# A fused decoder layer: the product of k and q stated at a later step, a sequence's prologue over two passes, a power one pass on

## The chip, the cores and the metric

The kernel is one program on one core of a Trainium2 chip. The metric is the device time of one execution in microseconds. The core has a matmul engine (TensorE; the profile tells its matmuls, PE, from its weight loads, PEld), three other compute engines (VectorE or DVE, ScalarE or ACT, GpSimd or POOL) and SyncE (SP), which here issues most of the DMAs. Every engine works through its own queue in order; engines wait for one another by semaphores.

## The reference

A decoder layer on x of shape (4, 512, 512): three residual blocks, each on a layer norm of x without weights. The first is a gated delta rule with 16 heads of 128, the second a cross attention to a context of 256 rows, the third an attention with a mixture of eight experts. The change lies in the first alone:

```python
q = _causal_conv(x @ Wq.T, cw_q, cb_q)      # four taps along the time, bias, silu
k = _causal_conv(x @ Wk.T, cw_k, cb_k)
v = _causal_conv(x @ Wv.T, cw_v, cb_v)
g = jnp.exp(-jnp.exp(A_log)[None, None, :] * jax.nn.softplus(a + dt_bias[None, None, :]))
beta = jax.nn.sigmoid(b)
q = _l2norm(q.reshape(Bb, Ss, H, DK))
k = _l2norm(k.reshape(Bb, Ss, H, DK))

def step(Sstate, inputs):
    q_t, k_t, v_t, g_t, beta_t = inputs
    retrieved = jnp.einsum('bhkv,bhk->bhv', Sstate, k_t)
    error = v_t - g_t[..., None] * retrieved
    update = k_t[..., :, None] * (beta_t[..., None] * error)[..., None, :]
    Snew = g_t[..., None, None] * Sstate + update
    o_t = jnp.einsum('bhkv,bhk->bhv', Snew, q_t)
    return (Snew, o_t)
```

a and b are two further projections of x to 16 columns each. The output o is normalised, gated by silu(x Wg) and projected by Wo.

## The kernel before, in words

The recurrence is computed in chunks of 128 time steps. A sequence of 512 steps has four chunks (TB), and the 16 heads are taken two at a time (HG = 2, so NHG = 8 groups). Four sequences times eight groups make 32 **passes**, numbered m from 0 to 31; "even" and "odd" below are by m.

Each pass m needs five pieces of work, each a Python generator that yields after every step, so that the pieces can be interleaved as the program is written out:

- `stage1(m)` (L534): the keys and queries of the two heads. k's projection and convolution (`conv`, L509: four matmul steps of L515, on ACT the last tap and the bias at L523, on DVE the three other taps at L526, on ACT Silu at L529), k's transposes (L558), the sums of its squares (L563) and their power on POOL (`rk`, L570), the decay matrix `em` (a scan on DVE at L579, scaled on ACT by `scale`, L397), k times k on PE (L588) and from it `at` (DVE, L591), which goes to DRAM. Then q: for each of the two heads its projection and convolution, `qg` (q times a row of decays, POOL, L602), q squared (ACT, L605), and the **product** of k and q: four pairs of matmuls (L612), multiplied by `em` on DVE into `pt` (L614). Last come the column sums of q squared (PE, L621; ACT, L623), which go by DMA into `rq` (L627), k decayed by chunk (`kdec`, L631 and L397) and the **power** of `rq` on POOL (L635, L636).
- `stage2_inverse(m)` (L649): a triangular inverse by elimination, 31 steps of two instructions each (L657, L658), on DVE for even m and on POOL for odd m, and its way through DRAM (L663 to L671).
- `stage2_values(m)` (L691): v's projection, convolution and transposes (L703, L705), the gate's projections (`conv` with m = 3, ACT at L519), and at its start the DMA of `rq` to DRAM (`r_d`, L696).
- `stage3(m)` (L721): the recurrence over the chunks: L735 to L769 finish the inverse; then per chunk L787 (k times state), L789 (`r`), L796 and L798 (`u`), L806, L809 and L811 (the next state), L814 and L816 (the output `po`). `stage3` reads `r_d` back (L773).
- `output(m)` (L841): the product with Wo (L860), summed over groups (L865).

`prologue(b)` (L405) prepares a sequence once: for each of its four tiles of 128 rows the layer norm (`layernorm`, L125: statistics on DVE at L131 and L132, `rsqrt` at L122 on DVE and L123 on POOL, normalising on DVE at L137), four transposes on PE (L427) and a copy on ACT (L428); then the two small projections (L435), softplus and the decays by a long row of small DVE operations (L438 to L483) with exponentials on ACT, and two rows of decays to DRAM (L493), which `stage1` reads back.

The main loop (L963) interleaves them. While `stage3(m)` takes its fifteen steps, after each of them one **turn** of the rest is taken: one step of `output(m - 1)`, two steps of `stage1(m + 2)`, one of `stage2_values(m + 1)`, two calls of `inversions` (the inverse of m + 1, and from about turn 10 on the first steps of that of m + 2), and in passes 4, 12 and 20 one step of the next sequence's prologue. What is left when `stage3(m)` is done is run to its end. For DVE and POOL the order so written is the order in which they work (L947: a manual schedule for these two); for PE and ACT the program's builder may move an instruction ahead of one written before it.

A step of `stage1` without work of its own ("yield" twice in a row) only puts distance between what stands before and behind it. Its 29 yields before fill the fifteen turns. In turn 9 q's first convolution ends, and in turn 10 its product is stated; in turns 11 and 12 the second head's projection and convolution, in turn 13 its product; in turn 14 the sums of squares, in turn 15 the end. PSUM tiles `pb` of the projections, transposes and products come from one pool of four.

Of the kernel before, what the change touches and what calls it, by code (L numbers as in the profile page):

```python
# [31 lines left out]
F32 = mybir.dt.float32  # L32
# [66 lines left out]
def decoder(ctx: ExitStack, tc: tile.TileContext, a: dict, out: bass.AP):  # L99
# [73 lines left out]
    def run(*gs):  # L173
        for g in gs:
            for _ in g:
                pass

    def turns(*gs):

# [146 lines left out]
    with ExitStack() as st:  # L326
# [78 lines left out]
        def prologue(b):  # L405

            x = []

            def load(c):

                t = w2.tile([P, D], F32, name="xa", bufs=4) if b == 0 and c > 1 else w2.tile([P, D], F32, name="x_in", bufs=2)
                nc.sync.dma_start(t, x_t[:, b * TB + c, :])
                x.append(t)

            for c in range(TB if b == 0 else 2):
                load(c)
            yield
            yield
            for c in range(TB):
                t = x[c]  # L420
                run(layernorm(t.unsqueeze(1), t.unsqueeze(1), small))
                if c == 0:
                    xnT = s2.tile([P, KD, S], F32, name="xnT", bufs=2)
                    seqs[b] = [xnT]
                tp = p_b.tile([P, KD, P], F32, name="pb")
                for kd in range(KD):
                    nc.tensor.transpose(tp[:, kd, :], t[:, kd * P : (kd + 1) * P], ident)  # L427
                nc.scalar.copy(xnT[:, :, c * P : (c + 1) * P], tp)  # L428
                if b > 0 and c + 2 < TB:
                    load(c + 2)  # L430
                yield
            pab = p_b.tile([P, TB, 32], F32, name="pb")
            for c in range(TB):
                for kd in range(KD):
                    nc.tensor.matmul(pab[:, c, :], xnT[:, kd, c * P : (c + 1) * P], wab[:, kd, :], start=kd == 0, stop=kd == KD - 1)  # L435
            g_a, lg, beta, gam, ngam, gend, gall = (seq.tile([P, H1, TB], F32, name=n) for n in ("g_a", "lg", "beta", "gam", "ngam", "gend", "gall"))
            nc.scalar.activation(beta, pab[:, :, 16:32].rearrange("p i h -> p h i"), AF.Sigmoid)
            nc.vector.tensor_tensor(g_a, pab[:, :, 0:16].rearrange("p i h -> p h i"), along(dtb, TB), ALU.add)  # L438


            y, z, w = (small.tile([P, H1, TB], F32, name=n, bufs=1) for n in ("sp_y", "sp_z", "sp_w"))
            nc.vector.scalar_tensor_tensor(y, g_a, -1.0, g_a, ALU.mult, ALU.min)
            nc.scalar.activation(y, y, AF.Exp)
            yield
            nc.vector.tensor_scalar(w, y, 2.0, None, ALU.add)
            nc.vector.reciprocal(w, w)
            nc.vector.tensor_tensor(z, y, w, ALU.mult)
            nc.vector.tensor_tensor(w, z, z, ALU.mult)
            nc.vector.tensor_scalar(y, w, 1.0 / 17, None, ALU.mult)
            for n in (15, 13, 11, 9, 7, 5, 3):  # L450
                nc.vector.scalar_tensor_tensor(y, y, 1.0 / n, w, ALU.add, ALU.mult)
                if n in (11, 5):
                    yield
            nc.vector.scalar_tensor_tensor(y, y, 1.0, z, ALU.add, ALU.mult)
            nc.vector.tensor_scalar(y, y, 2.0, None, ALU.mult)
            nc.vector.scalar_tensor_tensor(y, g_a, 0.0, y, ALU.max, ALU.add)
            nc.vector.scalar_tensor_tensor(y, y, -1.0, along(alog, TB), ALU.mult, ALU.mult)

            nc.vector.tensor_scalar(lg, y, -200.0, None, ALU.max)
            yield  # L460

            lgf = lg.rearrange("p h i -> p (h i)")
            pg = p_b.tile([P, 3, H1 * TB], F32, name="pb")
            for n, m in enumerate((C_UP, C_LO, C_ONE)):
                nc.tensor.matmul(pg[:, n, :], tab_a[:, m, :], lgf, start=True, stop=True)
            for n, dst in enumerate((gam, gend, gall)):
                nc.scalar.activation(dst.rearrange("p h i -> p (h i)"), pg[:, n, :], AF.Exp)
            nc.vector.tensor_scalar(ngam, gam, -1.0, None, ALU.mult)
            yield

            nc.vector.tensor_scalar(y, lg, -87.0, None, ALU.max)
            nc.vector.tensor_scalar(z, y, float(np.log2(np.e)), None, ALU.mult)
            nc.vector.tensor_scalar(z, z, MAGIC, MAGIC, ALU.add, ALU.subtract)
            nc.vector.scalar_tensor_tensor(y, z, -0.693145751953125, y, ALU.mult, ALU.add)
            nc.vector.scalar_tensor_tensor(y, z, -1.42860677e-06, y, ALU.mult, ALU.add)
            yield
            nc.vector.tensor_scalar(w, y, 1.0 / 5040, None, ALU.mult)
            for n in (720, 120, 24, 6, 2, 1):
                nc.vector.scalar_tensor_tensor(w, w, 1.0 / n, y, ALU.add, ALU.mult)
            n2 = small.tile([P, H1, TB], mybir.dt.int32, name="n2", bufs=1)  # L480
            nc.vector.tensor_scalar(n2, z, 127.0, None, ALU.add)
            nc.vector.tensor_scalar(n2, n2, 23, None, ALU.logical_shift_left)
            nc.vector.scalar_tensor_tensor(w, w, 1.0, n2.bitcast(F32), ALU.add, ALU.mult)  # L483
            yield

            tp = p_b.tile([H1 * TB, 2, P], F32, name="pb")
            nc.tensor.transpose(tp[:, 0, :], w.rearrange("p h i -> p (h i)"), ident)
            nc.tensor.transpose(tp[:, 1, :], gam.rearrange("p h i -> p (h i)"), ident)
            gr = w2.tile([P, TB * 64], F32, name="Y6").rearrange("p (n t) -> p n t", n=2)[0 : H1 * TB]
            nc.scalar.copy(gr, tp)  # L490
            nc.gpsimd.memset(gr[:, 0, 0:1], 0.0)
            for n in range(2):
                nc.sync.dma_start(g_d[b, n], gr[:, n, :])  # L493
            seqs[b] += [beta, gam, ngam, gend, gall]
            yield
# [38 lines left out]
        def stage1(m):  # L534
# [59 lines left out]
            load_blocks(m, ats)  # L594
            mb = rows(1)

            qg, pt, sq = [], [], []
            for p in range(HG):
                q = s1.tile([P, S], F32, name="qh")
                yield from conv(b, hg, p, 0, wq, q)  # L600
                g = live.tile([P, S], F32, name="qg", bufs=6)
                nc.gpsimd.tensor_tensor(g, q, mb[p], ALU.mult)  # L602
                qg.append(g)
                t = w2.tile([P, S], F32, name="cv", bufs=5)
                nc.scalar.activation(t, q, AF.Square)  # L605
                sq.append(t)
                yield
                yield
                pq = p_b.tile([P, TB, P], F32, name="pb")
                for c in range(TB):  # L610
                    cs = slice(c * P, (c + 1) * P)
                    nc.tensor.matmul(pq[:, c, :], kT[p][:, cs], q[:, cs], start=True, stop=True)  # L612
                t = live.tile([P, TB, P], F32, name="pt", bufs=6)
                nc.vector.tensor_tensor(t, pq, em[p], ALU.mult)  # L614
                pt.append(t)
                yield
            load_weights(m + 1, 0)

            pss = p_b.tile([P, S], F32, name="pb")
            for p in range(HG):  # L620
# [5 lines left out]
            for p in range(HG):  # L626
                nc.sync.dma_start(rq[p * P // HG : (p + 1) * P // HG, :], sr[p * 32 : p * 32 + 1, :].rearrange("o (n k) -> o n k", k=HG * TB))  # L627
            yield
            kd_ = []
            for p in range(HG):  # L630
                t = live.tile([P, TB, P], F32, name="kdec", bufs=4)  # L631
                scale(t, kt[p], ke, p)
                kd_.append(t)
                yield
            nc.gpsimd.tensor_scalar(rq, rq, 1e-24, None, ALU.max)  # L635
            nc.gpsimd.tensor_tensor(rq, rq, mhalf[:, 0 : HG * TB], ALU.pow)  # L636
            keys[m] = (kT, kd_, qg, pt, nr, rq)

        inverses, begun, joined = {}, {}, {}
# [51 lines left out]
        def stage2_values(m):  # L691
# [1 line left out]
            b, hg = divmod(m, NHG)  # L693
            nr, rq = keys[m][4:]
            wv, wg = weights.pop((m, 2)), weights.pop((m, 3))
            nc.sync.dma_start(r_d[m % SLOTS].rearrange("c t -> (c t)").rearrange("(n k) -> n k", k=HG * TB), rq)  # L696
            v_, gs = [], []
            for p in range(HG):
                t = yield from conv(b, hg, p, 2, wv, None)
# [4 lines left out]
                v = w2.tile([P, TB, P], F32, name="vn", bufs=4)  # L704
                nc.vector.tensor_tensor(v, tp, along(nr[:, p * TB : (p + 1) * TB], P), ALU.mult)  # L705
                v_.append(v)
                yield
            load_weights(m + 1, 2)
            for p in range(HG):
# [253 lines left out]
        for m in range(NP):  # L963
# [21 lines left out]
            if m + 1 < NP:  # L985
                rest.append((stage2_values(m + 1), 1))
                rest.append((inversions(m, turn), 2))
            if (m + 4) % NHG == 0 and (m + 4) // NHG < B:
                rest.append((prologue((m + 4) // NHG), 1))
            rest = turns(*rest)  # L990
            for _ in stage3(m):
                next(rest, None)
# [576 lines left out]
```

## Time and profile before

| | us |
|---|---|
| median of three runs | 3905.05 (3903.72 to 3906.9) |
| the profiled execution | 3901.65 |
| its span, first to last instruction | 3899.8 |
| start up to the first pass (first matmul of L735) | 156.0 |
| a pass, most of them | 61.3 to 61.7 |
| passes 4, 12 and 20, with a prologue | 90.5 to 90.6 |
| passes 8, 16 and 24 | 64.7 to 64.8 |
| pass 30, which has no more `stage1` | 39.1 |

The passes follow one another from 156 us on, and pass 31, the last, begins at 2132.0 us; the cross attention, the attention and the experts follow and are not touched. The page's row of PE's clock gives in tenths what the throttle granted over the span; slices 5, 10 and 15 hold the prologues:

```
PE   5898799897898899897898789999999999899897
PEclk8899899998999998999999799999999999999898
```

In the views below a row of a group of instructions reads: line, engine, operation, tile written and tiles read, shapes, count, then busy us and mean ns, then the idle time of the engine just before these instructions and what ended it. A row of a stretch reads: from and to, its length, the busy time of PE, PEld, DVE, ACT and POOL with the number of instructions, the granted clock (1.00 is full speed), the share of the DMA engines and GB/s. A row of the timeline reads: start, duration, engine, line, operation, tiles, count, and in brackets the idle time before it and its cause.

### The profile page before, as it was taken

The numbers are of one execution on the slowest core, as the hardware profiler recorded it, in microseconds if no ns is written. First come the engines' busy times: TensorE is split into PE (matmuls) and PEld (weight loads), VectorE is DVE, ScalarE is ACT, GpSimd is POOL, SyncE is SP. The second block draws the span as 40 slices with busy tenths as digits, with TensorE's granted clock in tenths as the row PEclk, the third lists the DMA queues.
The fourth block names the chain that finished last, engine by engine and source line by source line (L and its number), as shares of the span: only waits on it lengthen the run. The fifth ranks groups of instructions, "written<-read, shape, count | busy, mean of one in ns | idle before, by whom it ended". The sixth has DMA issues, their size and how long they took to land. (4 is left out here: it accounts for less than half of the span.)

```text
span 3899.8 us, 48830 instructions
## 1 busy us (share of the span) xinstructions
PE 3462.8 (89%) x16466; PEld 1967.7 (50%) x16466; DVE 2187.2 (56%) x4923; ACT 1566.2 (40%) x4379; POOL 1387.2 (36%) x1941
## 2 busy tenths in 40 slices
PE   5898799897898897899898789999999999899897
PEld 3555455554555554555555445555555555554343
DVE  5566566754765566566754446655665556554111
ACT  3444444443443444444443324444444444444121
POOL 1453453455255533553455222212211211211442
PEclk8899899998999998999999799999999999999898
DMA  5333233432334332334333155445544444456344
GB/s 151 99 107 112 84 94 107 129 94 87 104 100 127 96 101 86 108 93 131 103 97 110 43 176 159 138 135 155 166 143 144 144 142 133 139 169 213 79 83 92
DMA packets 391880, 465.56 MB, mean 119 GB/s; under 512 B 128451, under 2 KB 242115, under 8 KB 391440
## 3 DMA queue, kind: packets, MB, share of 16 engines
q1 hardware_dynamic: 380080, 438.03, 36.7%
q0 software_dynamic: 10112, 21.58, 2.9%
q8 instruction: 132, 2.16, 0.2%
q10 hardware_dynamic: 1440, 2.84, 0.2%
q14 instruction: 116, 0.95, 0.1%
HBM read 401.76 MB, written 64.81 MB: 120 GB/s over the span
## 5 line engine op out<-in xcount | busy, mean ns | idle before, releaser
L515 PE MATMUL pb<-xnT,w 128*128 128x512 f32 x2048 | 962.6, 608 | 18.4 <-DVE at L591 12.7
L515 PEld LDWEIGHTS pb<-xnT,w 128*128 128x128 f32 x2048 | 381.2, 197 | 426.8 <-issue 396.0
L526 DVE SCALAR_TENSOR_TENSOR cv<-pb,pp,cv 128x510 f32<-128x510 f32 (+2 forms) x576 | 423.5, 744 | 36.1 <-ACT cv L523 24.4
L1111 PE MATMUL pb<-c_q,hT 128*128 128x512 f32 x768 | 362.3, 610 | 10.9 <-DMA c_q<-in_c_wk_dram 3.3
L523 ACT ACTIVATE cv<-pb,pp 128x512 f32<-128x512 f32 x192 | 148.7, 775 | 374.2 <-PE pb L515 374.1
L658 POOL TENSOR_TENSOR iT<-iT,iW 32x31 f32<-32x31 f32 (+15 forms) x496 | 272.5, 549 | 38.9
L657 POOL TENSOR_TENSOR iW<-iA,iT 32x31 f32<-32x31 f32 (+15 forms) x496 | 246.3, 497 | 50.3 <-DMA iA<-at_d 9.6
L860 PE MATMUL pb<-wot,og 128*128 128x512 f32 x512 | 262.2, 636 | 1.5 <-issue 1.5
L602 POOL TENSOR_TENSOR qg<-qh,row 128x512 f32<-128x512 f32 x64 | 81.9, 1280 | 460.9 <-ACT qh L529 460.9
L1217 PE MATMUL pw<-c_o,oT 128*128 128x512 f32 x512 | 241.8, 603 | 2.9 <-DVE oT L1209 2.9
L1111 PEld LDWEIGHTS pb<-c_q,hT 128*128 128x128 f32 x768 | 144.3, 196 | 169.6 <-issue 152.3
L1183 ACT ACTIVATE e<-pb,nm,rq 128x128 f32<-128x128 f32 (+3 forms) x256 | 156.8, 618 | 140.5 <-DVE nm L1181 108.0
L570 POOL TENSOR_TENSOR rk<-ss,mhalf 128x8 f32<-128x8 f32 x32 | 87.1, 2722 | 346.9 <-DVE ss L569 346.0
L865 DVE TENSOR_TENSOR xa<-pb,xa 128x512 f32<-128x512 f32 x112 | 76.8, 686 | 219.2 <-PE pb L860 219.0
L657 DVE TENSOR_TENSOR iW<-iA,iT 32x31 f32<-32x31 f32 (+15 forms) x496 | 178.9, 361 | 28.4 <-DMA iA<-at_d 17.5
L658 DVE TENSOR_TENSOR iT<-iT,iW 32x31 f32<-32x31 f32 (+15 forms) x496 | 181.6, 366 | 17.1
L274 POOL TENSOR_SCALAR x_e<-x_e 128x1024 f32<-128x1024 f32 x64 | 67.4, 1053 | 331.2 <-ACT x_e L269 232.1
L1207 PE MATMUL po<-eT,val 128*128 128x512 f32 x320 | 170.2, 625 | 6.8 <-ACT eT L1205 3.8
L612 PE MATMUL pb<-qh,kT 128*128 128x128 f32 x512 | 97.3, 349 | 88.0 <-ACT qh L529 88.0
L1177 PE MATMUL pb<-kT,qT 128*128 128x256 f32 (+3 forms) x576 | 162.7, 409 | 0.8 <-ACT x_e L269 0.8
L269 ACT ACTIVATE x_e<-pb,nm 128x256 f32<-128x256 f32 x256 | 118.0, 476 | 96.5 <-DVE nm L266 96.5
L1039 POOL TENSOR_TENSOR rope_s<-q,tab 128x128 f32<-128x128 f32 x64 | 35.2, 550 | 316.2 <-DVE q L1141 270.1
(331 smaller groups left out, 6576.1 us busy)
## 6 DMA issues: line engine op xcount, KB each, us to landing
c_o<-in_c_wo_dram SPq DMA_DIRECT2D x128, 512.0 KB, 4.1
c_q<-in_c_wq_dram SPq DMA_DIRECT2D x128, 512.0 KB, 4.7
w<-in_a_w_dram SPq DMA_DIRECT2D x124, 512.0 KB, 3.9
row<-g_d SPq DMA_DIRECT2D x64, 512.0 KB, 3.5
at_d<-at SPq DMA_DIRECT2D x64, 256.0 KB, 2.2
T<-t_d SPq DMA_DIRECT2D x32, 512.0 KB, 4.1
X<-x_d SPq DMA_DIRECT2D x32, 512.0 KB, 5.2
wot<-in_a_wo_dram SPq DMA_DIRECT2D x32, 512.0 KB, 3.6
```

The source lines that it names most:

```text
L269: nc.scalar.activation(e[:, n, :], ps[r][:, g, :], AF.Exp, bias=nm[:, n : n + 1], accum_out=ssum[:, n : n + 1])
L515: nc.tensor.matmul(pj, wt[:, kd, p * P : (p + 1) * P], xnT[:, kd, :], start=kd == 0, stop=kd == KD - 1)
L523: nc.scalar.activation(ac, pj, AF.Identity, bias=cb[:, m, h : h + 1], scale=cw[:, m, h, 3:4])
L526: nc.vector.scalar_tensor_tensor(ac[:, j:], pj[:, : S - j], cw[:, m, h, 3 - j : 4 - j], ac[:, j:], ALU.mult, ALU.add)
L657: eng.tensor_tensor(u, A[:, i, i + 1 :].unsqueeze(2).to_broadcast([nb, n, w]), T[:, i, :w].unsqueeze(1).to_broadcast([nb, n, w]), ALU.mult)
L658: eng.tensor_tensor(T[:, i + 1 :, :w], T[:, i + 1 :, :w], u, ALU.add)
L860: nc.tensor.matmul(pw, og[p][:, c * P : (c + 1) * P], wot[:, p, :], start=p == 0, stop=p == HG - 1)
L1111: nc.tensor.matmul(pj, hT[:, kd, :], w[:, kd % 2, :], start=kd == 0, stop=kd == KD - 1)
L1177: nc.tensor.matmul(ps[:, m, k * P : (k + w) * P], qT[g][:, n + m, :], kT[:, g, j : j + w, :], start=True, stop=True)
L1183: nc.scalar.activation(e[n + m][:, :nk], ps[:, m, :nk], AF.Exp, bias=nm[:, n + m : n + m + 1], scale=rq, accum_out=es[:, n + m : n + m + 1])
L1207: nc.tensor.matmul(po, val[:, g, :], eT, start=k == 0, stop=k == c)
L1217: nc.tensor.matmul(pw, oT[:, h + m, :], w[:, m, :], start=g == 0 and h + m == 0, stop=g == 3 and h + m == 3)
```

## The change

It has four parts.

1. In `stage1` the product becomes a function and is stated at another place. The first head's stands in the second head's convolution, behind its projection and ahead of its taps (the third step of `conv`); the second head's stands behind the column sums of q squared. The two steps without work go, so `stage1` has 26 yields in place of 29. `kdec` is stated one head at a time, the first ahead of the column sums, and the load of q's next weights comes two turns earlier.
2. The power of `rq` moves out of the end of `stage1(m)` into `stage2_values(m)`, behind the first head's v, that is into turn 5 of the next pass, and the DMA of `rq` to `r_d` moves with it from turn 1.
3. For the sequences after the first, the prologue's steps are drawn out: the statistics of a tile, its normalising and its transposes stand in different turns, and the small DVE operations are cut into more steps. For the first sequence the statistics of all four tiles stand ahead of the first normalising.
4. The prologue runs in passes 4, 12 and 20 only as long as `stage3` has turns left (`within`, which stops when the list `turn` is emptied) and goes on in passes 5, 13 and 21. With one step a turn the four tiles' transposes are stated in the first pass, and everything from L435 on in the second, up to its turn 12.

```diff
+    def within(g, turn):
+
+        while turn and next(g, g) is not g:
+            yield
...
             yield
             yield
+            norms_of = [layernorm(t.unsqueeze(1), t.unsqueeze(1), small) for t in x]
+            for g in norms_of[: TB if b == 0 else 1]:
+                next(g)
+            if b:
+                yield
             for c in range(TB):
                 t = x[c]
-                run(layernorm(t.unsqueeze(1), t.unsqueeze(1), small))
+                run(norms_of[c])
+                if b:
+                    yield
+                    if c + 1 < TB:
+                        next(norms_of[c + 1])
+                    yield
...
                 if b > 0 and c + 2 < TB:
                     load(c + 2)
+                    norms_of.append(layernorm(x[c + 2].unsqueeze(1), x[c + 2].unsqueeze(1), small))
                 yield
...
             for n in (15, 13, 11, 9, 7, 5, 3):
                 nc.vector.scalar_tensor_tensor(y, y, 1.0 / n, w, ALU.add, ALU.mult)
-                if n in (11, 5):
+                if n in (15, 11, 7, 3):
                     yield
...
             for n in (720, 120, 24, 6, 2, 1):
                 nc.vector.scalar_tensor_tensor(w, w, 1.0 / n, y, ALU.add, ALU.mult)
+                if n in (24, 1):
+                    yield
...
-            qg, pt, sq = [], [], []
+            qh, qg, pt, sq, kd_ = [], [], [], [], []
+
+            def product(p):
+                pq = p_b.tile([P, TB, P], F32, name="pb")
+                for c in range(TB):
+                    cs = slice(c * P, (c + 1) * P)
+                    nc.tensor.matmul(pq[:, c, :], kT[p][:, cs], qh[p][:, cs], start=True, stop=True)
+                t = live.tile([P, TB, P], F32, name="pt", bufs=6)
+                nc.vector.tensor_tensor(t, pq, em[p], ALU.mult)
+                pt.append(t)
+
+            def decayed(p):
+                t = live.tile([P, TB, P], F32, name="kdec", bufs=4)
+                scale(t, kt[p], ke, p)
+                kd_.append(t)
+
             for p in range(HG):
                 q = s1.tile([P, S], F32, name="qh")
-                yield from conv(b, hg, p, 0, wq, q)
+                c = conv(b, hg, p, 0, wq, q)
+                yield from itertools.islice(c, 2)
+                if p:
+                    product(0)
+                yield from c
+                qh.append(q)
...
                 sq.append(t)
                 yield
-                yield
-                pq = p_b.tile([P, TB, P], F32, name="pb")
-                for c in range(TB):
-                    cs = slice(c * P, (c + 1) * P)
-                    nc.tensor.matmul(pq[:, c, :], kT[p][:, cs], q[:, cs], start=True, stop=True)
-                t = live.tile([P, TB, P], F32, name="pt", bufs=6)
-                nc.vector.tensor_tensor(t, pq, em[p], ALU.mult)
-                pt.append(t)
-                yield
             load_weights(m + 1, 0)
+            decayed(0)
+            yield
...
             yield
-            kd_ = []
-            for p in range(HG):
-                t = live.tile([P, TB, P], F32, name="kdec", bufs=4)
-                scale(t, kt[p], ke, p)
-                kd_.append(t)
-                yield
-            nc.gpsimd.tensor_scalar(rq, rq, 1e-24, None, ALU.max)
-            nc.gpsimd.tensor_tensor(rq, rq, mhalf[:, 0 : HG * TB], ALU.pow)
+            product(1)
+            yield
+            decayed(1)
+            yield
             keys[m] = (kT, kd_, qg, pt, nr, rq)
...
-            nc.sync.dma_start(r_d[m % SLOTS].rearrange("c t -> (c t)").rearrange("(n k) -> n k", k=HG * TB), rq)
...
                 v_.append(v)
+                if p == 0:
+                    nc.gpsimd.tensor_scalar(rq, rq, 1e-24, None, ALU.max)
+                    nc.gpsimd.tensor_tensor(rq, rq, mhalf[:, 0 : HG * TB], ALU.pow)
+                    nc.sync.dma_start(r_d[m % SLOTS].rearrange("c t -> (c t)").rearrange("(n k) -> n k", k=HG * TB), rq)
                 yield
...
+
             if (m + 4) % NHG == 0 and (m + 4) // NHG < B:
-                rest.append((prologue((m + 4) // NHG), 1))
+                coming = prologue((m + 4) // NHG)
+                rest.append((within(coming, turn), 1))
+            elif (m + 3) % NHG == 0 and (m + 3) // NHG < B:
+                rest.append((coming, 1))
```

## The prediction

> **What bounds the kernel now.** I read the page first, then the granted clock by stretches, then TensorE's waits over the delta rule's passes, then the order of time inside a pass. The kernel before has 32 passes (one sequence and two heads each); in the trace a pass begins at the first matmul of L735, at 733.9, 795.5, 857.2 us and so on. The page:
>
> ```profile
> span 3899.8 us, 48830 instructions
> PE 3462.8 (89%) x16466; PEld 1967.7 (50%) x16466; DVE 2187.2 (56%) x4923; ACT 1566.2 (40%) x4379; POOL 1387.2 (36%) x1941
> L612 PE MATMUL pb<-qh,kT 128*128 128x128 f32 x512 | 97.3, 349 | 88.0 <-ACT qh L529 88.0
> ```
>
> TensorE (PE) is the bound, and the product of k and q waits 88.0 us for q's Silu. The chain that ended last covers only the closing DMAs and says nothing here. The waits of PE from 156 to 2093 us (total, times, longest):
>
> ```profile
> PE pb L612 <- ACT qh L529: 77.2, 42, 2.7
> PE pb L427 <- DVE x_in L137: 49.8, 12, 7.4
> PE ps L806 <- ACT u L798: 36.8, 24, 2.7
> PE ps L787 <- DVE state L811: 21.7, 20, 1.4
> ```
>
> The change touches the first two. Four passes (length; PE, PEld, DVE, ACT and POOL busy; clock; DMA): odd, even, even with a prologue, the odd one behind it:
>
> ```profile
> 733.90:795.50 61.60, 55.69 (x301) 32.45 (x301) 42.47 (x87) 26.28 (x77) 19.64 (x30) 0.97 0.38 112
> 795.50:857.20 61.70, 55.19 (x298) 32.39 (x298) 34.94 (x70) 26.20 (x77) 39.70 (x59) 0.97 0.35 103
> ...
> 918.60:1009.20 90.60, 69.44 (x353) 43.16 (x352) 46.70 (x115) 36.88 (x92) 41.43 (x64) 0.87 0.27 83
> 1009.20:1071.60 62.40, 56.20 (x301) 32.67 (x302) 44.63 (x91) 26.09 (x77) 21.21 (x31) 0.95 0.34 101
> ```
>
> A prologue makes its pass 28.9 us longer than an even one and its clock 0.87. Where the clock goes:
>
> ```profile
> 772.00:775.70 3.70, 0.75 (x4) 0.56 (x4) 3.63 (x8) 0.60 (x1) 0.00 (x0) 1.00 0.70 166
> 775.70:779.40 3.70, 3.62 (x17) 3.62 (x18) 1.17 (x3) 1.70 (x5) 2.46 (x6) 0.54 0.80 193
> ...
> 832.10:837.05 4.95, 2.34 (x16) 1.96 (x16) 4.84 (x9) 1.42 (x4) 3.41 (x3) 1.00 1.03 242
> 837.05:840.60 3.55, 3.55 (x17) 3.55 (x18) 1.09 (x3) 1.66 (x4) 2.50 (x2) 0.54 0.51 147
> ...
> 942.40:949.20 6.80, 6.73 (x29) 3.99 (x29) 0.83 (x3) 1.58 (x4) 2.67 (x5) 0.50 0.12 39
> ```
>
> Behind the wait at the first product (2.46 us in both passes) PE runs at 0.54 for some 3.6 us: the product takes 1.98 us, the one at 788.9 only 1.11. So that wait costs 2.46 + 0.46 x 3.6 = 4.1 us.
>
> **Part A: the product is stated later.** Nothing is added or removed on PE, ACT or DVE; the order changes. Before, q's second projection (eight matmuls of L515) stands behind the first product; now it stands ahead of it, and the second product stands behind the sums of squares (L621). The 27 passes 0 to 29 without a prologue have the 4.1 us: 15 odd, 12 even. Even ones also wait 0.76 at the second product. What is late next:
>
> Odd pass, from the product at L787 (772.57): L787 0.6, eight matmuls at 5.36/12 = 0.45 each 3.6, L796 0.6, the first product 1.1: 778.5. Then on DVE pt (L614) 0.69 and three taps 2.3, on ACT Silu 0.63 and Square 0.63, handovers 0.3: 783.0. PE meanwhile has the transposes of v 0.65, half a gate projection 1.8, L806/L814/L816 1.3: 782.3. If L621 is next it waits 0.7, if the gate's other half (1.8), not at all. With L621 (1.05) and that half done PE stands at 785.1 to 785.9; before, it ends that half at 787.67 and L621 would be done at 788.7. Gain 2.8 to 3.6; I take 3.0, near the lower since what is stated first usually goes first.
>
> Even pass: DVE is held up by something that the change leaves, the landing of the next inverse's blocks:
>
> ```profile
> 836.85 0.60 DVE L789 SCALAR_TENSOR_TENSOR r<-ps,ngam,vn 128x128 f32<-128x128 f32 x2
> 837.05 1.83 PE L612 MATMUL pb<-qh,kT 128*128 128x128 f32 x8 [2.46 <-ACT qh L529]
> ...
> 842.34 0.18 DVE L657 TENSOR_TENSOR iW<-iA,iT 32x31 f32<-32x31 f32 x1 [1.02 <-DMA iA<-at_d]
> ```
>
> Two steps of the inverse stand there ahead of pt and q's taps in DVE's written order: 842.34 + 0.9 + 0.69 + 2.3 + 0.62 + 0.63 + handovers 0.3 = 847.8. PE, from 834.59: 3.6 + 0.6 + 0.65 + 1.1 + 1.8 + 1.3 + 1.8 = 10.9, so 845.5, and waits 2.3. What is then left (L621 1.05, L787 0.6, second product 1.1, gate 3.6, L796 0.6, L814/L816 0.9: 7.9) ends at 855.7; before, the next pass began at 857.2. Gain 1.5.
>
> A = 15 x 3.0 + 12 x 1.5 = 63 us. Bounds: 15 x 2.5 + 12 x 0.5 = 44 if handovers take twice as long and the blocks land 1 us later; 15 x 3.6 + 12 x 3.2 (both waits gone, clock unchanged) = 92.
>
> **Part B: the prologue over two passes.** Of the 28.9 us, PE's work at full clock is 16 transposes 2.6 (four take 0.65 at L558), L435 3.65, L465 0.78, L487/L488 0.3: 7.3. The other 21.6 is waits and slow clock. The first tile:
>
> ```profile
> 934.68 0.15 DVE L122 TENSOR_SCALAR rsq<-ln_mv 128x1 f32<-128x1 f32 x1
> 940.94 0.56 POOL L123 TENSOR_TENSOR ln_rs<-rsq,mhalf 128x1 f32<-128x1 f32 x1
> 941.54 0.88 DVE L137 TENSOR_SCALAR x_in<-x_in,ln_mv,ln_rs 128x512 f32<-128x512 f32 x1 [6.71 <-POOL ln_rs L123]
> 942.47 1.11 PE L427 MATMUL pb<-tab,x_in 128*128 128x128 f32 x4 [7.38 <-DVE x_in L137]
> ```
>
> The power stands on POOL behind the inverse, DVE waits 6.71 for it, PE 7.38, and then 3.34, 3.06, 2.76 for the other tiles. Now normalising is a turn (61.6/15 = 4.1 us) behind the statistics and the transposes one or two more. POOL's lag there falls too: the power of q's sums (L635, L636: 0.25 + 1.67 + gaps 0.16 = 2.1 us), which stood ahead of this in the same unbroken run of POOL, goes behind it. 940.94 - 2.1 = 938.8 is ahead of the turn's end (in an undisturbed even pass DVE ends turn 4 at 818.1, 22.6 into the pass, here 941.2). So these waits go.
>
> What comes: the second half (L435 to L491) lands in the odd pass behind, whose DVE has no break from 742.7 to 766.2. It adds some 8.6 us of small DVE operations (0.2 to 0.25 each, L451's seven 1.8); PE brings 3.65 + 0.78 = 4.4 of its own, so up to 4.2 shows; I take 4. In the even pass two powers of 0.56 stand ahead of rk (L570): 1. Then 28.9 - 7.3 - 5 + 1.5 (A's gain, which this pass now has too) = 18.1, x 3 = 54 us. Bounds: no cover, 9.7 in place of 5: 40; all but 1 covered: 66.
>
> **Moved at no cost.** The power (now turn 5 of the next pass): in odd passes POOL idles 22 us ahead of rk; in even ones it stays within the same run ahead of rk, so rk's time stands; without that cover it is 2.1 x 12 = 25 us. The DMA of it to r_d moves past wot's load on SP; behind it in turn 5 is only at's store, not ready before 830.8. The row is read a pass later. q's weights are loaded two turns earlier, once L515 is done. kdec (L397) runs at 846.2 already, ahead of its place in the text.
>
> Rule against row: POOL's rk takes 1.65 us alone and 3.61 beside DVE's scan, whose own 1.17 does not grow; so a power beside DVE's two-input steps costs POOL time, not DVE. [...]
>
> **Part C: the start.** Prologue 0 has twelve steps in place of eight beside k's projections; on DVE the second k's taps now stand ahead of the exponentials (35.3 to 38.8), which end up to 5 us later. Against it two product waits there (6.36 and 3.94). Net between -5 and +10; I take 0.
>
> **Sum.** 63 + 54 + 0 = 117; 3901.65 (span 3899.8 and 1.85 around it) - 117 = 3785. The median of the runs is 3.4 above the profiled execution: 3788. All bounds: gain 79 to 168, so 3737 to 3826.
>
> **Rivals.**
> 1. The wait only moves: L621 stands one turn behind Square as the product stood one turn behind Silu. PE's order is also not wholly the text's (kdec), so it may fall back. Then A is 12 x 0.76 = 9: 3905 - 9 - 54 = 3842. Against it: eight matmuls (3.6 us) now stand between. 15%.
> 2. The prologue's waits move into the odd pass; only its slow clock comes back: L860 11.37 against 7.83, L427 3.95 against 2.6, L796 and L767 0.9: 5.8 x 3 = 17, so 3905 - 63 - 17 = 3825. 12%.
> 3. The slow clock stays, as other waits remain in those turns (L806 2.68, L787 1.40): 27 x 1.65 = 45, so 3833. Against it: behind the lone 2.68 at 832.1 the clock was 1.00. [...] 8%.
> 4. Slower: in DVE's written order pt now stands ahead of q's taps. If PE reaches the product late, taps 2.3, Silu and Square 1.25, state, r and u 1.7 and six handovers 0.6 lie bare where nothing fills PE: 5.9 + slow clock 1.6 = 7.5 in 27 passes, 203. Against the waits removed (27 x 4.4 = 119) and B 54: 3934. It decides from 6.4 us a pass; the eight matmuls make PE late by 3.6 only. 9%.
> 5. Gains and losses cancel: 3905, 3%.
>
> The forecast has 53%; its own range is 3745 to 3825. The range 3737 to 3850 takes in rivals 1 to 3. This kernel's runs lie within 3.2 us; 0.2% (8 us) is what can be told from no change: faster 88%, within 3%, slower 9%.
>
> **What will show it.** PE's wait at the product near 0, no 0.54 stretch behind it; a wait at L621 under 1 us in odd and about 2 in even passes; odd passes 58.6, even ones 60.2; a prologue's two passes about 133 in place of 153; L427's waits gone after the start. Wrong if L621 or L787 takes over the 2.46, or if the odd pass behind a prologue exceeds 70.

## The result, and the profile after

The changed kernel takes 3777.2 us (median of four runs, 3771.8 to 3784.6) against 3906.0 us for the kernel before in the same session: a ratio of 0.9672 with a 95% interval of 0.9654 to 0.9689. The forecast was 3788 us with a range of 3737 to 3850. The profiled execution took 3776.1 us, 125.9 us less in its span than the one before.

The page after (span; then busy us, share of the span and number of instructions of each engine):

```profile
span 3773.9 us, 48783 instructions
PE 3437.1 (91%) x16466; PEld 1917.6 (51%) x16466; DVE 2189.5 (58%) x4923; ACT 1559.3 (41%) x4379; POOL 1383.9 (37%) x1941
```

DVE, ACT and POOL are as busy as before to 7 us. PE's busy time fell by 25.7 us though it runs the same 16466 matmuls: part of the gain is not idle time but a faster clock (granted on the mean 0.98 in place of 0.95 below). Passes 2 to 29 as one stretch, before and after (length; PE, PEld, DVE, ACT, POOL busy; clock; DMA):

```profile
270.20:2092.90 1822.70, 1601.96 (x8482) 943.16 (x8481) 1132.92 (x2311) 765.91 (x2201) 855.37 (x1262) 0.95 0.35 102
262.30:1969.80 1707.50, 1580.89 (x8485) 896.96 (x8487) 1134.91 (x2311) 759.73 (x2201) 852.92 (x1262) 0.98 0.36 109
```

Of the 115.2 us that went here, 94.1 were idle time of PE and 21.1 busy time. The waits of PE over the passes (147.9 to 1969.8 us; total, times, longest):

```profile
PE ps L836 <- ACT u L828: 47.5, 24, 3.6
PE pb L576 <- ACT kT L547: 17.1, 30, 2.8
PE pb L621 <- ACT qh L547: 15.5, 14, 1.2
PE pb L533 <- DVE at L609: 13.4, 3, 4.5
PE pb L481 <- DVE lg L475: 12.5, 3, 5.0
```

L621 is the product (L612 before): 15.5 us of waits are left of 77.2. The prologue's transposes, 49.8 before, are gone from the list. The largest wait is now one that the change left alone (L836, L806 before) and that grew from 36.8 to 47.5. The four passes that were shown before, an odd one, an even one, one with a prologue and the odd one behind it (length; PE, PEld, DVE, ACT, POOL busy; clock; DMA):

```profile
694.20:751.90 57.70, 55.02 (x297) 30.54 (x296) 43.37 (x90) 25.93 (x77) 19.44 (x29) 1.00 0.41 123
751.90:812.50 60.60, 55.87 (x297) 31.82 (x296) 35.05 (x67) 26.04 (x77) 40.15 (x60) 0.97 0.35 105
870.30:933.00 62.70, 57.46 (x317) 33.24 (x320) 37.67 (x81) 27.60 (x80) 42.05 (x64) 0.97 0.39 115
933.00:1003.40 70.40, 63.30 (x341) 37.69 (x341) 52.41 (x125) 34.99 (x89) 19.29 (x30) 0.93 0.27 79
```

The odd pass is 3.9 us shorter, with the clock at 1.00 all through. The two passes of a prologue together take 133.1 in place of 152.9. Within the odd pass (PE and ACT alone; start, duration, engine, line, what):

```profile
732.83 0.75 PE L817 MATMUL ps<-state,kT 128*128 128x128 f32 x4 [0.53 <-DVE state L841]
733.41 2.74 PE L533 MATMUL pb<-xnT,w 128*128 128x512 f32 x6
735.35 0.63 ACT L547 ACTIVATE qh<-cv 128x512 f32<-128x512 f32 x1 [4.74 <-DVE cv L544]
...
737.71 1.06 PE L621 MATMUL pb<-qh,kT 128*128 128x128 f32 x8
...
741.75 1.04 PE L652 MATMUL pb<-cv,tab_a 128*32 128x512 f32 x2
...
743.78 1.05 PE L652 MATMUL pb<-cv,tab_a 128*32 128x512 f32 x2
```

The same product and sums of squares in the odd pass before:

```profile
775.78 1.98 PE L612 MATMUL pb<-qh,kT 128*128 128x128 f32 x8 [2.46 <-ACT qh L529]
...
791.68 1.05 PE L621 MATMUL pb<-cv,tab_a 128*32 128x512 f32 x4
```

Two of the second projection's eight matmuls even went ahead of L817; the other six fill the time until Silu ends at 735.98, and the product runs in 1.06 us and not in 1.98. The two heads' sums of squares (L652, L621 before) wait for nothing, since two of the gate's matmuls stand between them. But this parting has a price. Standing together, the four matmuls of the sums took 1.05 us; parted, each head's two take as long alone. PE's and PEld's busy time on that line in the odd pass, before and after:

```profile
733.90:795.50 61.60, 1.05 (x4) 0.14 (x4) 0.97 0.38 112
694.20:751.90 57.70, 2.09 (x4) 0.27 (x4) 1.00 0.41 123
```

So each pass costs PE 1.04 us more, 29.1 us over passes 2 to 29. All other matmuls there took 50 us less (21.1 and 29.1), at a granted clock of 0.98 in place of 0.95.

### The profile page after: what moved, and what is told of

Same layout as the page of the kernel before. It is cut to its first block, busy times and chain, and to the rows that moved or that the text cites. A ratio compares the mean times of both kernels' runs of the same rounds, so it can differ in the third digit from the quotient of the medians.

```text
span 3773.9 us, 48783 instructions
## 1 busy us (share of the span) xinstructions
PE 3437.1 (91%) x16466; PEld 1917.6 (51%) x16466; DVE 2189.5 (58%) x4923; ACT 1559.3 (41%) x4379; POOL 1383.9 (37%) x1941
## 5 line engine op out<-in xcount | busy, mean ns | idle before, releaser
L533 PE MATMUL pb<-xnT,w 128*128 128x512 f32 x2048 | 974.5, 610 | 18.4 <-DVE at L609 13.9
L533 PEld LDWEIGHTS pb<-xnT,w 128*128 128x128 f32 x2048 | 373.6, 195 | 407.8 <-issue 384.2
L890 PE MATMUL pb<-wot,og 128*128 128x512 f32 x512 | 252.3, 616 | 2.0 <-issue 1.5
L685 DVE TENSOR_TENSOR iT<-iT,iW 32x31 f32<-32x31 f32 (+15 forms) x496 | 192.0, 387 | 17.1
L402 ACT ACTIVATE em<-em,ee 128x128 f32<-128x128 f32 x256 | 78.3, 388 | 178.3 <-POOL ee L590 108.5
```

What stands on the lines that cost most here:

```text
L533: nc.tensor.matmul(pj, wt[:, kd, p * P : (p + 1) * P], xnT[:, kd, :], start=kd == 0, stop=kd == KD - 1)
L685: eng.tensor_tensor(T[:, i + 1 :, :w], T[:, i + 1 :, :w], u, ALU.add)
L890: nc.tensor.matmul(pw, og[p][:, c * P : (c + 1) * P], wot[:, p, :], start=p == 0, stop=p == HG - 1)
```

## The experiments

Medians are of one session each, with the kernel before beside them (3902.4 to 3906.9). Pass lengths are from the profiled executions.

**a_only: the order of stage1 alone.** The kernel before with part 1 of the change; prologue and power as before.

> The kernel before with the new order of stage1 alone (product, kdec, q's weights); the prologue runs in one pass as before and the power of q's sums stays at the end of stage1. Theory: the 4.1 us behind the first product fall away by 3.0 in odd and 1.5 in even passes, 63 us by the working of part A; the passes of the changed kernel show some 56, so 3843 to 3852. The passes with a prologue keep about 90 us and their clock of 0.87. Rival (the wait at the product only moves, and the prologue brought nearly all): above 3890.

Measured: 3821.4 us, ratio 0.9786 (0.9768 to 0.9805), 85 us less, some 22 more than the forecast for it. Eleven undisturbed odd passes fell from 61.47 to 57.78, the eleven even ones without a prologue from 62.55 to 61.39 on the mean, the start up to the first pass from 156.0 to 145.7, and each prologue's two passes by 5.8 to 7.9. The prologue's own waits are all there:

```profile
PE pb L432 <- DVE x_in L137: 52.5, 12, 7.9
PE ps L822 <- ACT u L814: 41.5, 24, 3.3
PE pb L608 <- ACT qh L534: 15.0, 11, 2.3
```

(L432 is L427, L608 the product.) The rival, that the wait only moves, is out.

**prod_ahead: the changed kernel with the first product ahead of q's second projection.**

```diff
-                c = conv(b, hg, p, 0, wq, q)
-                yield from itertools.islice(c, 2)
                 if p:
                     product(0)
-                yield from c
+                yield from conv(b, hg, p, 0, wq, q)
```

> The changed kernel with the first head's product stated ahead of q's second projection, half a turn behind q's Silu, the second head's left where it is. Theory: the eight matmuls of the projection (3.6 us) that stand between are what hides Silu; without them PE waits for it in each of 28 passes as before the change, at least 2.46 us, with 1.65 us of slow clock behind it, 4.1 x 28 = 115 at the most, less what the new order of the second head keeps: 3830 to 3890. Rival (PE is given another order by the program's builder, or the second head's place is what counts): 3770 to 3790.

Measured: 3891.8 us, ratio 0.9973 (0.9961 to 0.9984). One move of four pairs of matmuls gives back 115 of the 129 us. PE's waits over its passes:

```profile
PE pb L621 <- ACT qh L547: 60.7, 27, 2.5
PE ps L834 <- ACT u L826: 45.3, 24, 3.3
PE ps L815 <- DVE state L839: 18.0, 14, 1.4
```

The product waits 2.5 us again, and the clock falls with it: in passes 2 to 29 the records of the granted clock hold 198.0 us at half speed, against 68.3 in the changed kernel and 180.9 in the one before. The result lies 1.8 us above the expected range: odd and even passes away from a prologue (62.35 and 63.72 on the mean) are even longer than before the change (61.47 and 62.55). The sums of squares are parted here too (66.4 us on their line in this trace, 33.7 before); no run shows that this is the reason.

**b_only: the prologue's new steps and its two passes alone.**

> The kernel before with the prologue's new steps and its spread over two passes alone; stage1 and the power as before. Theory: 28.9 us more in each of three passes become 7.3 of PE work and some 5 of new waits, so 50 us less, 3850 to 3862, with about 137 us for a prologue's two passes. If the two parts simply add, this gain and that of the run with the order alone make the 129 us of the whole but for 8 us that the start brings. Rival (the prologue's waits go away only because the product leaves room or because the power has left POOL): 3880 or more.

Measured: 3872.1 us, ratio 0.9907 (0.9891 to 0.9924), 35 us less, less than expected. The pairs of passes take 141.2 to 142.0 in place of 152.7 to 152.9, and the even pass behind each pair is longer (65.0, 63.0 and 63.8 in place of 61.7).

**power_back: the changed kernel with the power of q's sums where it was.**

```diff
-                if p == 0:
-                    nc.gpsimd.tensor_scalar(rq, rq, 1e-24, None, ALU.max)
-                    nc.gpsimd.tensor_tensor(rq, rq, mhalf[:, 0 : HG * TB], ALU.pow)
-                    nc.sync.dma_start(r_d[m % SLOTS]...)
```

(They stand at the end of `stage1` and at the head of `stage2_values` again.)

> The changed kernel with the power of q's sums back at the end of stage1 and its DMA to r_d back at the head of the values. Theory: in even passes the power stands in the same unbroken run of POOL ahead of rk in both places, so rk's time stands and nothing changes but 1 to 2 us in each pass with a prologue (the first tile's power is 2.1 us later): 3775 to 3786. Rival (the power at the end of stage1 waits there for its DMA and holds POOL's inverse): 10 to 30 us slower than the changed kernel, 3787 to 3807.

Measured: 3793.0 us, ratio 0.9712 (0.9691 to 0.9732), 16 us slower than the changed kernel; the theory's upper end was 3786. The time fits the rival, but its mechanism does not show: POOL does wait for that DMA (3.0 us at the end of an even pass), yet rk starts 31.6 us into an ordinary even pass against 31.5, so its time stands nearly as forecast, and the wait at L836 is 3.2 against 3.07. (Behind a prologue rk is 0.7 later.) Half speed is granted for 99.0 us in place of 68.3 in passes 2 to 29, and of the 15.1 us that these passes are longer, 10.5 are busy time of PE on the same matmuls and 4.6 idle time. That a wait of one length can have both outcomes is seen in two even passes, the first of a_only, the second of power_back:

```profile
802.81 0.71 PE L822 MATMUL ps<-u,kdec 128*128 128x128 f32 x4 [3.27 <-ACT u L814]
...
765.60:825.60 60.00, 54.71 (x300) 30.66 (x299) 34.52 (x65) 26.12 (x77) 42.30 (x62) 1.00 0.35 106
```

```profile
793.55 1.22 PE L835 MATMUL ps<-u,kdec 128*128 128x128 f32 x4 [3.26 <-ACT u L827]
...
756.30:818.20 61.90, 56.98 (x301) 32.80 (x303) 33.69 (x67) 26.10 (x77) 42.21 (x62) 0.94 0.35 103
```

Both wait 3.3 us; in the second the matmuls behind it run at half speed (1.22 against 0.71), and the pass is 1.9 us longer. What differs is where the wait falls. In the traces of the kernel before and of the changed kernel slow stretches begin whole multiples of 3.413 us apart (at 704.23, 714.47, 775.91 and 837.35 before; at 789.93, 909.39, 964.01 and 974.25 after), so windows of that length can be laid end to end over a trace from the start of a slow stretch. Such windows around the two waits, a_only first:

```profile
797.71:801.13 3.42, 1.83 (x5) 0.53 (x3) 0.33 (x1) 1.64 (x6) 2.95 (x8) 1.00 0.00 0
801.13:804.54 3.41, 1.60 (x12) 1.42 (x12) 2.84 (x6) 2.46 (x7) 2.95 (x7) 1.00 0.61 159
```

```profile
788.94:792.35 3.41, 1.35 (x4) 0.28 (x2) 0.69 (x1) 2.11 (x8) 2.86 (x9) 1.00 0.00 0
792.35:799.18 6.83, 5.63 (x19) 4.59 (x20) 6.03 (x11) 3.30 (x9) 4.96 (x8) 0.50 0.81 192
```

In a_only the wait is split between two windows, and PE is busy for 1.83 and 1.60 us of them; in power_back most of it falls into one, PE is busy for 1.35 us, and half speed follows. Over passes 2 to 29 of the kernel before and of the changed kernel, such a window at full speed with PE busy for less than 0.40 of it was followed by half speed in 48 of 48 cases, with 0.40 to 0.50 in 5 of 26, and with more in 2 of 885.

**power_t10: the power five turns later still.** In the same lines `if p == 0` becomes `if p == 1`.

> The changed kernel with the power of q's sums and its DMA five turns later, behind the second head's v (turn 10 in place of turn 5). There POOL idles in odd passes (3.5 us ahead of qg) and has ended its inverse in even ones. Theory: the largest wait that is left on PE, L836 behind u (47.5 us in 24 waits, 3.07 us in even passes), comes from rk's place at the end of POOL's run, so with 2.1 us less in that run rk comes 2.1 us earlier in 15 even passes, and the slow clock behind that wait (0.58 for 4 us) goes too: 25 to 43 us less, 3735 to 3755. Rival (the even pass is set by the landing of the next inverse's blocks or by DVE, not by rk): no change, 3770 to 3785.

Measured: 3752.7 us, ratio 0.9610 (0.9594 to 0.9626): 24 us less than the changed kernel. In an even pass (rk, the scaling of em, L836):

```profile
773.38 1.65 POOL L588 TENSOR_TENSOR rk<-ss,mhalf 128x8 f32<-128x8 f32 x1
775.63 2.45 ACT L402 ACTIVATE em<-em,ee 128x128 f32<-128x128 f32 x8 [5.47 <-POOL ee L590]
...
778.95 0.71 PE L836 MATMUL ps<-u,kdec 128*128 128x128 f32 x4 [1.15 <-ACT u L828]
```

The pass begins at 743.8, so rk comes at 29.5 in place of 31.5, and the wait is 1.15 in place of 3.07. The eleven even passes fall from 61.19 to 58.94 on the mean.

**one_pass: all of the prologue's steps in one pass, two a turn.** `rest.append((prologue((m + 4) // NHG), 2))` in place of `within` and `coming`.

> The changed kernel with the prologue's 27 steps all in passes 4, 12 and 20, two a turn. Theory: what counts is a turn between statistics, normalising and transposes; two steps of one turn stand directly behind one another, so the first tile waits for POOL's power again (6 us with its slow clock) and others in part; DVE's small operations fall into the same pass: 5 to 10 us more for each prologue, 3790 to 3808. Rival (the second pass is what counts, its lack brings back what the prologue cost): pass 4 near 87, 12 to 15 us more for each, 3813 or more. Third: half a turn is enough, and one pass costs nothing: 3770 to 3785.

Measured: 3780.2 us, ratio 0.9684 (0.9668 to 0.9701); the interval overlaps that of the changed kernel. The pairs take 133.5, 133.0 and 132.8, as 75.3 and 58.3 in place of 62.4 and 69.0. The third possibility held: the second pass brings nothing. PE's waits in the first prologue's pass, where L442 are the transposes (L427 before):

```profile
PE pb L533 <- ACT xnT L443: 3.1, 1, 3.1
PE pb L442 <- DVE x_in L137: 1.6, 1, 1.6
PE pb L505 <- DVE sp_w L501: 1.5, 1, 1.5
```

**norm_together: statistics directly ahead of normalising again**, for the sequences after the first.

```diff
-            for g in norms_of[: TB if b == 0 else 1]:
+            for g in norms_of[: TB if b == 0 else 0]:
...
-                    if c + 1 < TB:
-                        next(norms_of[c + 1])
```

> The changed kernel, but for the sequences after the first a tile's statistics stand directly ahead of its normalising again; the turns between normalising and transposes, the smaller steps and the two passes stay. Theory: DVE in its written order waits for POOL's power behind the inverse again (6.7 us at the first tile before, less 2.1 for the power that has left POOL's run, 0.7 to 3.5 at the others), but the transposes stand one turn or two behind, so PE feels it only where DVE's other work is late by it: 3 to 8 us a prologue, 3786 to 3801. Rival (the turn between statistics and normalising is what brought it all): the waits at the transposes come back, 12 us or more a prologue, 3813 or more. Third (the turns ahead of the transposes are enough): 3770 to 3784.

Measured: 3784.8 us, ratio 0.9692 (0.9673 to 0.9710); the interval overlaps that of the changed kernel. The profile tells a little more: the pairs take 134.6, 136.3 and 136.3 against 131.3, 133.1 and 134.6, so 2.7 us a prologue. In the passes the transposes wait nowhere over 1.6, but the projection behind them waits 3.3 for their copy in the first prologue's pass. So the turn ahead of normalising is worth little. That the turns between normalising and transposes carry the rest is argued by elimination; no run takes them alone away.

**t10_pg: an empty step ahead of the prologue's matmuls for the decays**, on top of power_t10.

> The kernel with the power at turn 10 (3752.7), and one step without work ahead of the prologue's matmuls for the decays, so that they are stated a turn behind the last of DVE's operations that they read. Theory: the wait there (3.6 to 5.0 us in passes 5, 13 and 21, with slow clock behind it) is the same mistake as the product's before the change, and goes: 5 to 7 us in three passes, 3731 to 3738. Rival (PE has nothing else to do there, or the gap moves to the transposes): 3748 to 3757.

Measured: 3746.4 us, ratio 0.9597 (0.9581 to 0.9613), not to be told from power_t10 alone; it lies between what the theory and the rival gave. In pass 5 of the changed kernel and of this one:

```profile
PE pb L481 <- DVE lg L475: 5.0, 1, 5.0
PE pb L576 <- ACT kT L547: 2.8, 1, 2.8
```

```profile
PE pb L578 <- ACT kT L549: 2.8, 1, 2.8
PE ps L828 <- DVE r L821: 2.5, 2, 2.1
```

The wait at the decays' matmuls is gone, and 2.5 us of it come back at u's matmuls (L828, which wait for r on DVE): the rival held in the main.

**both: power_t10 with the next inverse a turn later on DVE.** `if turn and loaded > 4` becomes `if turn and loaded > (4 if m % 2 else 6)`.

> The kernel with the power at turn 10 (3752.7), and in even passes the next inverse's first steps one turn later on DVE (from turn 11). Theory: DVE no longer stands still for the landing of the inverse's blocks (2.13 us in turn 10 of even passes) ahead of pt and q's taps, so the wait at the second product (1.2 us) and what follows it go: 1 to 1.7 us in 14 even passes, 3728 to 3742. Rival (DVE's inverse then ends later in odd passes and T and X come late): waits of PE at the first matmul of a pass, 3755 to 3790.

Measured: 3748.3 us, ratio 0.9608 (0.9591 to 0.9624), no gain that can be told. The profile shows two halves that cancel: even passes 57.15 in place of 58.94, odd ones 59.13 in place of 57.78. In an odd and in an even pass PE waits for

```profile
PE ps L826 <- DVE r L819: 2.1, 2, 1.8
PE ps L836 <- ACT u L828: 0.9, 1, 0.9
...
PE ps L836 <- ACT u L828: 1.1, 1, 1.1
PE pb L576 <- ACT kT L547: 0.3, 1, 0.3
```

The second product's wait has left the even pass, as the theory had it. In the odd pass DVE ends its inverse a turn later and r stands behind it; T and X were not late, so the rival's cost came, though by another way.

**best and best2: both theories' halves together.** best adds to t10_pg the later start on DVE, with the steps that this puts off to be made up in turn 14.

> The kernel with the power at turn 10 and the step ahead of the prologue's matmuls for the decays (3746.4), and in even passes the next inverse's first steps from turn 11 on with one more in each of turn 14's two calls, so that as many are done by the pass's end as before. Theory: even passes as in the run with the later start (57.2 us in place of 59.0), odd ones as without it (57.8 in place of 59.1, as DVE has no more steps there): 14 x 1.7 = 24 us less, 3715 to 3732. Rival (the steps moved to turn 14 hold DVE's work at the end of the pass): odd passes again 59 and no gain, 3740 to 3752.

Measured: 3751.6 us, ratio 0.9607 (0.9586 to 0.9628), odd passes 59.5. The steps were never made up: the count by which turn 14 was told stands still once the inverse has begun. best2 counts calls:

```diff
-                if turn and loaded > 4:
-                    next(begun.setdefault(m + 2, stage2_inverse(m + 2)), None)
+                if turn and loaded > (4 if m % 2 else 6):
+                    for _ in range(2 if m % 2 == 0 and n in (27, 28) else 1):
+                        next(begun.setdefault(m + 2, stage2_inverse(m + 2)), None)
```

> The kernel with the power at turn 10, the step ahead of the prologue's matmuls for the decays, and in even passes the next inverse's first steps from turn 11 on, now with the two steps that this puts off really made up in turn 14 (told by the count of calls, as the other count stands still once the inverse has begun, so that in the run named best no step was added). Theory: even passes 57.0 to 57.5 us, odd ones back at 57.8 from 59.5, as DVE again ends its inverse in turn 8 and r in turn 10 is not behind it: 11 odd passes and three behind a prologue times 1.5 = 21 us less than the run named best (3751.6) and some 15 to 20 less than the one with the power at turn 10 alone (3752.7), 3728 to 3740. Rival (it is the shorter even pass itself that makes DVE late in the odd one, not the number of steps): odd passes 59 again, 3742 to 3752.

Measured: 3723.4 us, ratio 0.9536 (0.9523 to 0.9549): 54 us less than the changed kernel and the fastest of all. An odd and an even pass of it:

```profile
683.00:740.80 57.80, 55.09 (x297) 30.57 (x296) 44.55 (x93) 25.86 (x77) 19.16 (x29) 1.00 0.46 135
740.80:797.20 56.40, 54.50 (x301) 30.64 (x304) 34.56 (x65) 25.96 (x77) 40.12 (x60) 1.00 0.38 113
```

Even passes keep their 56.4 (57.35 over eleven), odd ones are back at 57.78: it was the number of DVE's steps left for the odd pass that held r.

## Why the prediction was right

By the spans of the two profiled executions, term by term (forecast gain, measured gain in us):

| | forecast | measured |
|---|---|---|
| eleven odd passes away from a prologue (61.47 to 57.76) | 33 | 40.9 |
| eleven even passes without a prologue (62.55 to 61.19) | 16.5 | 15.0 |
| three prologues, two passes each (458.4 to 399.0) | 63 | 59.4 |
| start (156.0 to 147.9) | 0 | 8.1 |
| passes 0 and 1 | 4.5 | -0.3 |
| pass 30 and all behind it | 0 | 2.7 |
| sum | 117 | 125.8 |

So the forecast of the time was right, and most of its parts by passes too. What stands behind the parts is less even, as the experiments show.

**Part A, the product stated later: right in its mechanism, too small, and with one cost missed.** The eight matmuls of the second projection are what hides Silu (prod_ahead). "Nothing is added or removed on PE" did not hold: the sums of squares, counted at 1.05 us, take 2.09 in two halves, 1.04 us a pass. Other things brought more than that. An odd pass gains 3.7 and not 3.0: the working let PE follow the written order at the sums of squares and took nothing for the wait at L787, but the projection filled part of that wait too (1.40 before, 0.53 after). An even pass gains 1.4 against 1.5. The bound named for even passes, DVE's wait for the landing of the inverse's blocks, is there:

```profile
799.42 0.18 DVE L684 TENSOR_TENSOR iW<-iA,iT 32x31 f32<-32x31 f32 x1 [2.13 <-DMA iA<-at_d]
...
805.05 0.94 PE L621 MATMUL pb<-qh,kT 128*128 128x128 f32 x6 [1.21 <-ACT qh L547]
```

Only the 2.3 us that were foreseen at the sums of squares show as 1.2 at the second product, and taking the blocks out of the way (both, best2) removes them. Two terms were missed on the other side: the order also shortens the start by 10 us (part C, put at 0 with an upper bound of 10) and the two passes of each prologue by 20.4 in all, where 13.5 had been counted (4.5 of it in part B). With the longer gain of the odd passes these make the step from 63 to a_only's 85 us, less what the even passes and passes 0 and 1 fall short there.

**Part B, the prologue: right that its waits go, and by the distances that it named, but too large.** one_pass has the same time without the second pass, so the spread over two passes, for which the part is named, brought nothing that can be told. The gain is 35 us alone (b_only) or 28 on top of the new order (a_only against power_back), not 54. The term that was mis-sized is "5 of new waits": the two passes of a prologue in power_back take 134.2, which is 14.2 more than an odd and an even pass of the same kernel without one (57.8 and 62.2 on the mean). With the 7.3 of matmuls that leaves 6.9 in place of 5, some 6 us over three prologues. Pass 5 of the changed kernel, shown above, has 5.0 of waits at the decays' matmuls and 2.8 at k's transposes. The rest is not of the prologue's making: 4.5 of the 54 were A's gain; A's order alone had taken 5.8 to 7.9 us from each pair, where 4.5 (3.0 and 1.5) had been counted, some 7 us; and the eleven even passes away from a prologue are 9 us longer in power_back than in a_only (62.22 against 61.39 on the mean).

**The power: "moved at no cost" missed 16 us.** rk's place did stand, to 0.1 us (31.6 and 31.5). Of the 15.1 us in passes 2 to 29, 11.3 are in the eleven even passes away from a prologue and 3.6 in the pairs. The 0.15 us on a wait of 3.2 cannot be the whole reason, since a_only has waits of 3.2 to 3.3 at the same place and even passes of 61.39, close to the 61.19 of the changed kernel. Where such waits fall in these windows differs between a_only and power_back, as shown; how much of the 16 us belongs to the power's place and how much to this chance, no run separates. That the 16 and A's surplus made up for B, so that the sum came out closer than its terms, is luck.

**The clock: the reading was right and carried some two fifths of the result.** Half speed went from 180.9 to 68.3 us in passes 2 to 29. Half of the 112.6 us would be 56, but PE idles in part of such stretches: it was busy for 155.5 us of them before and for 62.1 after, and half of that difference is 47. This agrees with the 50 us that the matmuls other than the sums of squares took less, of the 115 that these passes lost. In these passes, before and after, slow stretches last 3.41 us or a multiple. Waits of 2.46 us before the change, and of 3.26 in power_back, were each followed by one. Rival 3 was therefore rightly put low.

**The other rivals.** Rival 1 fell with a_only. Rival 2, the waits that move into the odd pass, came true in part, with 5.0 and 2.8 us there. Rival 4 stayed out: PE reached the product at 737.7, behind which q's taps took 2.3 us of DVE with PE busy.

What stays open: the time from the start of pass 31 on, where nothing was changed, lies between 1763 and 1773 us in these kernels, and no run here told why. Nor did a run put the sums of squares together again in the new order, which might bring some of their 1.04 us a pass back.

## What to carry to other kernels

Where the engine that bounds the time waits a little at the same place in every pass, look for independent work that is already in the program and state it between producer and consumer; the length of that work against the length of the chain says beforehand what it brings. Price such a wait with the slow matmuls behind it, which here cost some two thirds of the wait again (1.65 us on 2.46, an estimate from the clock of 0.54 over 3.6 us before the change), and expect it to be paid in some passes and not in others: here half speed followed a wait of 3.26 us and not one of 3.27. Before other work is put into a group of matmuls, look whether its members cost less together than apart (here 1.05 us for four matmuls together, 2.09 in two halves). And where an engine works in written order, look for what stands in its queue ahead of the late operation: moving one power of 2 us out of POOL's run, and two elimination steps from one turn of DVE to another, brought 54 us on top of the change, together with one empty step in the prologue that alone could not be told from nothing.

## What the runs showed of the hardware that was not expected

A wait of 3.27 us left the clock at 1.00 in one even pass and a wait of 3.26 us brought it to half for a stretch in another, 60.0 against 61.9 us for the same work. The two differed not in the wait's length but in PE's busy time in the windows of 3.413 us laid over the traces: 1.35 us of it were followed by half speed, 1.60 and 1.83 us were not. Four matmuls of the sums of squares, two for each head with 32 columns of weights each, took 1.05 us together, and two of them alone 1.04 us; apart they cost PE 2.09. And an elementwise step on POOL beside DVE's scan of em took 1.26 and 1.32 us in an even pass of the changed kernel (at 778.58 and 779.91, 32x175), where its neighbours took 0.50 and 0.59 (32x192) and 0.44 and 0.48 (32x156), while the scan's pair took 2.58 us, against 2.34 in the start (at 49.76) with no instruction of POOL beside it and 2.32 beside rk's power: in this pass both took longer, POOL by far the more. The prediction took from a row that a power beside the scan costs POOL time and not DVE; but in that row the scan began first (761.90, the power 762.06), so it shows that order and that operation of DVE alone.
